# A macaron block on one core: each attention step's third maximum cut into two half-length pieces that share a bank, the two row halves of the array shifted against each other, and the transposed maxima sent to their rows by transfers inside SBUF

## The chip, the cores and the metric

The kernel runs on one core of a Trainium2 chip. The metric is the device time of one execution in microseconds (us); lower is better. Every profile that is shown is that of one execution.

## The reference

The block works on `x` of 4 batches x 1024 rows x 512 columns. It adds half of a feed-forward of the normalised rows, then attention of the normalised rows, then half of the same feed-forward again. What the change touches is the softmax of the attention (32 query heads, 8 key heads, 16 columns to a head, so 4 query heads to a key head):

```python
scores = jnp.einsum('bhqd,bhkd->bhqk', Q, K) / np.sqrt(HD).astype(np.float32)
w = jax.nn.softmax(scores, axis=-1)
attn = jnp.einsum('bhqk,bhkd->bhqd', w, V)
...
x = x + 0.5 * _L0_ffn_ref(_layernorm(x, axis=-1), L0_ffn_w_gate_up, L0_ffn_w_proj)
x = x + _L0_attn_ref(_layernorm(x, axis=-1), ...)
x = x + 0.5 * _L0_ffn_ref(_layernorm(x, axis=-1), L0_ffn_w_gate_up, L0_ffn_w_proj)
```

A softmax subtracts each row's maximum before it takes the exponential. The kernel computes the scores twice: once laid out with queries on the partitions, only to find each query's maximum, and once transposed, with keys on the partitions, for the exponential.

## The kernel before, in words

The program alternates between a feed-forward stage (`FeedForward`, its steps called pieces) and an attention stage for each of the four batches. Within both the order of instructions is written out by hand (`manual_schedule`); each engine then runs its own list in that order and waits on semaphores.

**The attention stage** is `Attention.run`. It has 128 steps per batch: 8 key heads `g`, for each two halves of the queries `qh`, for each eight tiles of 128 keys `kc`. One step `n` does this:

- `scores`, twice, for the head pairs 0 and 1 (the tiles `s`, L1273). Each pair is two TensorE matmuls with a contraction of 64 rows, 512 columns wide; one uses the upper 64 rows of the array, the other the lower 64, so that they run beside each other. The tile `s` of a pair has one place in PSUM, and the step of the next keys adds to what is there. So a pair's matmuls in step n+1 wait until the exponential of that pair in step n has read `s`. Where `kc` is 0, two more matmuls per pair add the negated maxima (`pick` times `even_rows` or `odd_rows`).
- the exponentials on ScalarE (the tiles `e`, L1282), one of 1024 columns per pair.
- three maxima for a key head that is computed later (`maxima`, tiles `sm`, L1138): a matmul with a 64-row contraction and 512 columns, and its reduction on VectorE (L1147). Two of them stand behind the first pair of scores, one in each row half. The third stands behind the second pair of scores, in one row half; the other half has nothing beside it.
- `weigh` (tiles `o`, L1289) for the step before: the exponentials times the values, four matmuls 32 columns wide, each in two passes.

**Where the maxima go.** Some of the maxima of a batch, 168 of 512, are computed in the feed-forward pieces ahead of its attention stage (`early`, in groups of four, up to the limit `EARLY`). When a key head has all of its maxima, VectorE reduces them to 32 numbers for each query row and splits these into two parts (`subtract_maxima`, L1169 to L1173). TensorE transposes them (`turn`, L1181), VectorE copies them out, GpSimd's queue writes them to DRAM (`d_m`, L1185) and reads them back as rows (`maxima_in`, L1221). The last two key heads take another way, without DRAM (`turn_half`): four transposes of 128x128 (L1208) and a copy of 512 columns (L1209), for four query tiles at a time.

**`divide`** ends a pair of key heads, 32 steps. The outputs `oT` go to DRAM (`d_o`), the denominators come back (`den`, on SyncE's queue). Three pieces of work then wait in the list `after`, and the step loop takes them out 7, 12 and 15 steps later: `invert` (VectorE's reciprocal, a write to `d_r`, and GpSimd's load of `aT` from `d_o`, L1085), `spread` (SyncE's load of `rec` from `d_r`, 512 KB, L1088) and `multiply` (GpSimd, `aT` times `rec`, L1091). With the first three `divide`s of a batch taken up in steps 32, 64 and 96, `multiply` is given out in steps 47, 79 and 111. The fourth is done behind the loop.

**Loads.** `Places` keeps four sets of three SBUF tiles for the queries and keys of a key head, one kind for maxima (`p_m`) and one for scores (`p_s`). `done` sets a place free, and the next load in a fixed order is issued on SyncE's queue, three transfers of 512 KB.

Of the kernel before, what the change touches and what calls it, by code (L numbers as in the profile page):

```python
# [19 lines left out]
P = 128  # L20
# [5 lines left out]
PAIR = 64  # L26
# [11 lines left out]
def tile_macaron_block(  # L38
# [21 lines left out]
    KV = HKV * HD  # L60

# [744 lines left out]
    def output(old, put, then, wp, ps):  # L806
        for i in range(NT):
            put.bias(i)
            put(i, range(DC - 1))
            if i == 3 or i == NT - 1:  # L810

                for _ in range(2 if i == 3 else 1):
                    old.after.pop(0)()
        turns = []
        for some in ([0, 1], [2, 3]):
            for i in some:
                put(i, range(DC - 1, DC))
            scales = normal_scales(then.tiles(0, some), f"last_{some[0]}")
            turns += then.normalize(0, some, wp, ps, "pa", 4, scales, NT)

        ends = []
        for i in range(4, NT):
            put(i, range(DC - 1, DC), ends)
        for step in turns + ends:
            step()

    def input_output(new, old, put, then, wp, ps):
        turn, banks = None, 2 if put is None else 1
        puts = {4: (0,), 5: (1,), 6: (2,), 7: (3,), 8: (4,), 9: (5, 6, 7)}
        for n in range(NT + 2):  # L830
# [40 lines left out]
            if put is not None and n == 3:  # L871
                old.after.pop(0)()
# [24 lines left out]
    class Attention:  # L897
# [19 lines left out]
        READY = (HKV - 1) * STEPS + NT - 3  # L917
        FIRST = 3
        EARLY = (3 * ITEMS - 4) * G

        def __init__(self, b):
            self.b = b


            self.d_q = dram.tile([D, 2, T], F32, tag="d_q", name=f"d_q_{b}", bufs=2)
            self.d_k = {
                kind: dram.tile([KV, 2, 2, T], F32, tag=f"d_k{kind}", name=f"d_k{kind}_{b}", bufs=2)
                for kind in "ms"
            }
            self.d_o = dram.tile([HQ, 2, HD, T], F32, tag="d_o", name=f"d_o_{b}", bufs=2)  # L930
            self.aT, self.after, self.when = {}, [], 0
            self.counts, self.ended = [0] * G, [0] * G
            self.pm, self.mT, self.mrows = {}, {}, {}
            self.early_rows = None
            self.rows, self.xTs, self.made = {}, {}, {}
            self.turning = []
# [132 lines left out]
        def divide(self, c, wp):  # L1069
# [20 lines left out]
            def multiply():  # L1090
                nc.gpsimd.tensor_tensor(a, a, rec, ALU.mult)  # L1091
                self.aT[c] = a

            self.after += [invert, spread, multiply]
# [31 lines left out]
        def maxima(self, j, ps, bufs):  # L1126

            g, n = divmod(self.counts[j], self.ITEMS)
            self.counts[j] += 1
            i, half = divmod(n, 2)  # L1130
            *q, k = places.at["m", self.b, g]
            if g not in self.pm:
                self.pm[g] = ring.tile([P, NT, G, 2], F32, tag="pm", name=f"pm_{self.b}_{g}")
            pm = self.pm[g]
            tag = "sm" if bufs < 4 else "gu"
            s = ps.tile([P, 512], F32, tag=tag, name=f"sm_{self.b}_{g}_{j}_{n}", bufs=bufs)
            at = slice(j % 2 * PAIR, (j % 2 + 1) * PAIR)
            nc.tensor.matmul(  # L1138
                s,
                lhsT=q[j // 2][at, i * P : (i + 1) * P],  # L1140
                rhs=k[at, half * 512 : (half + 1) * 512],
                start=True,
                stop=True,
            )

            def end():
                nc.vector.tensor_reduce(pm[:, i, j, half : half + 1], s, AX.X, ALU.max)  # L1147
                before = min(self.ended)
                self.ended[j] += 1
                done, rest = divmod(min(self.ended), self.ITEMS)  # L1150
                if min(self.ended) == before:
                    return
                if rest == self.ITEMS // 2 and g == HKV - 1:
                    self.turn_half(g, 0)
                elif rest == 0:
                    if g < HKV - 2:
                        self.subtract_maxima(g, ps, bufs)
                    else:
                        for part in range(g == HKV - 1, 2):
                            self.turn_half(g, part)  # L1160
                    places.done(("m", self.b, g))

            return end

        def subtract_maxima(self, g, ps, bufs):

            b = self.b
            m = small.tile([P, NT, G], F32, tag="m", name=f"m_{b}_{g}", bufs=2)
            nc.vector.tensor_reduce(m, self.pm[g], AX.X, ALU.max, negate=True)  # L1169
            mst = small.tile([P, G, 2, NT], F32, tag="mst", name=f"mst_{b}_{g}", bufs=2)  # L1170
            by_head = m.rearrange("p i j -> p j i")
            nc.vector.tensor_copy(mst[:, :, 0, :].bitcast(F32R), by_head)
            nc.vector.tensor_tensor(  # L1173
                mst[:, :, 1, :].bitcast(F32R), by_head, mst[:, :, 0, :], ALU.subtract
            )
            rows = G * 2 * NT
            tag = "sm" if bufs < 4 else "gu"

            def turn():
                pt = ps.tile([P, 512], F32, tag=tag, name=f"pmT_{b}_{g}", bufs=bufs)  # L1180
                nc.tensor.transpose(pt[:rows, :P], mst.rearrange("p j r i -> p (j r i)"), ident)  # L1181
                mrow = small.tile([rows, P], F32R, tag="mrow", name=f"mrow_{b}_{g}", bufs=2)
                nc.vector.tensor_copy(mrow, pt[:rows, :P])
                self.mT[g] = dram.tile([rows, P], F32, tag="d_m", name=f"d_m_{b}_{g}", bufs=HKV)
                nc.gpsimd.dma_start(self.mT[g], mrow.bitcast(F32))  # L1185
                if g == 0:
                    self.maxima_in(g)

            self.turning.append(turn)

        def turn_half(self, g, part):

            tiles = slice(part * 4, part * 4 + 4)
            m = small.tile([P, 4, G], F32, tag="m", name=f"m_{self.b}_{g}_{part}", bufs=2)
            nc.vector.tensor_reduce(m, self.pm[g][:, tiles], AX.X, ALU.max, negate=True)
            columns = self.spread[:, tiles].rearrange("p i (e s) -> p i e s", s=PAIR)[..., :4]
            high, low = (columns[..., r::2] for r in range(2))
            m = m.rearrange("p i (a e) -> p i e a", e=2)  # L1200
            nc.vector.tensor_copy(high.bitcast(F32R), m)
            nc.vector.tensor_tensor(low.bitcast(F32R), m, high, ALU.subtract)

            def turn():
                t = self.mrows[g] = self.odd_rows if g % 2 else even_rows
                pt = self.ps.tile([P, 512], F32, tag="sm", name=f"pmT_{self.b}_{g}_{part}", bufs=3)
                for i in range(4):
                    nc.tensor.transpose(pt[:, i * P : (i + 1) * P], self.spread[:, part * 4 + i, :], ident)  # L1208
                nc.vector.tensor_copy(t[:, part * 512 : (part + 1) * 512], pt)  # L1209

            self.turning += [None, turn] if g == HKV - 1 else [turn]

        def maxima_in(self, g):
# [5 lines left out]
            for j in range(G):  # L1219
                at = j % 2 * PAIR + j // 2 * 2  # L1220
                nc.gpsimd.dma_start(t[at : at + 2, :].bitcast(F32), flat[j])  # L1221

        def early(self, ps, share, more):
# [14 lines left out]
            if more and sum(self.counts) + G <= min(share, 1.0) * self.EARLY:  # L1238
                ends = [self.maxima(sum(self.counts) % G, ps, 4) for _ in range(G)]
# [10 lines left out]
        def run(self, keep, wp, ps):  # L1250
# [3 lines left out]
            self.spread = wp.tile([P, NT, P], F32, tag="spread", name=f"spread_{b}", bufs=1)  # L1254
# [4 lines left out]
            def scores(g, qh, kc, pair):  # L1259
# [10 lines left out]
                for n, (lhsT, rhs) in enumerate(terms):  # L1270
                    for e in range(2):
# [8 lines left out]
                        )  # L1280
                w = wp.tile([P, 2, 512], F32, tag="e", name=f"e_{name}", bufs=4)
                return w, lambda: nc.scalar.activation(w, s, AF.Exp, scale=1.0 / HD**0.5)  # L1282
# [27 lines left out]
            pattern = [((0, 1), (2,)), ((3, 0), (1,)), ((2, 3), (0,)), ((1, 2), (3,))]  # L1310
            more = (0, 5, 10, 15)
            late = None
            places.load(("t2", b + 1) if b + 1 < B else ("out", B))
            for n in range(HKV * self.STEPS):
# [3 lines left out]
                if n % self.STEPS > 0 and g + 1 < HKV and g + 1 in self.mT and g + 1 not in self.mrows:  # L1318
                    self.maxima_in(g + 1)
                if self.after and n in (self.when + 7, self.when + 12, self.when + 15):  # L1320
# [6 lines left out]
                sides = list(pattern[n % 4]) if n > 0 else [(), ()]  # L1327
                if n > 0 and n % 16 in more and self.TOTAL - sum(self.counts) > 3 * (self.READY - n):
                    sides[1] += (sides[1][0] ^ 1,)
                es, ends = {}, []  # L1330
                for pair, heads in enumerate(sides):
                    es[pair], end = scores(g, qh, kc, pair)
                    ends.append(end)
                    for j in heads:
                        if self.counts[j] < HKV * self.ITEMS:
                            ends.append(self.maxima(j, ps, 3))
                for end in ends:
                    end()
# [6 lines left out]
                if n == 1:  # L1345
                    nc.gpsimd.memset(self.spread, 0.0)
# [111 lines left out]
```

## Time and profile before

| | us |
|---|---|
| median of 3 runs | 3197.84 (3196.88 to 3199.02) |
| the profiled execution, its own time | 3200.95 |
| its span from the first to the last instruction | 3199.2 |
| TensorE busy in it | 3112.0 (97%) |
| VectorE, ScalarE, GpSimd busy | 2188.1, 1758.5, 951.0 |

How to read it: in the waits, "A <- B: total, times, longest" says that A's engine stood idle until B ended. A timeline line gives the start, the length and the instruction, merged with equal ones next to it (xN); what stands in brackets is the idle time ahead of it and who ended it. PE is TensorE's matmuls, PEld its weight loads, DVE VectorE, ACT ScalarE, POOL GpSimd, SP SyncE. The ends of matmuls are modelled and each overlaps the next, so what counts for TensorE is the distance from start to start. In a row of windows, each engine's busy time stands in this order: PE, PEld, DVE, ACT, POOL, then the granted clock of TensorE, the DMA share and GB/s.

### The profile page before, as it was taken

What the parts mean: (1) busy time and instruction counts of PE and PEld (TensorE: products, weight loads), DVE (VectorE), ACT (ScalarE), POOL (GpSimd) and SP (SyncE); (2) the same over time, 40 slices, a digit from 0 to 9 for tenths busy, and PEclk for the clock granted to TensorE, in tenths of its full rate; (3) what the DMA queues carried; (4) which work ended last, traced back from release to release, by engine and by line L of the source; (5) the groups of instructions that cost most, each with busy time, mean ns of one, the idle gap of its engine ahead of it and who ended that gap; (6) DMA issues with size and microseconds to landing.
All of it is one profiled execution on the core that took longest, in us unless ns stands there. A gap on an engine that the chain in (4) does not pass through costs nothing. (4 is left out here: it accounts for less than half of the span.)

```text
span 3199.2 us, 46128 instructions
## 1 busy us (share of the span) xinstructions
PE 3112.0 (97%) x16944; PEld 1963.6 (61%) x16944; DVE 2188.1 (68%) x3659; ACT 1758.5 (55%) x2346; POOL 951.0 (30%) x932
## 2 busy tenths in 40 slices
PE   5999899999999999999999999999999999999999
PEld 4777677733358777533377777433487776333687
DVE  7976566588855666688756665888556666887243
ACT  5752333389852333689823333898623335888343
POOL 2564333300034343201053333110243332010344
PEclk8999999999999999999999999999999999999999
DMA  3543222224324133133333222133241231332111
GB/s 111 161 125 97 88 61 78 62 76 120 111 82 129 53 93 109 45 117 102 91 107 96 87 73 70 70 110 115 86 130 60 76 96 61 97 120 65 41 60 42
DMA packets 229522, 285.64 MB, mean 89 GB/s; under 512 B 29296, under 2 KB 174704, under 8 KB 229296
## 3 DMA queue, kind: packets, MB, share of 16 engines
q1 hardware_dynamic: 220784, 271.66, 27.4%
q0 software_dynamic: 8512, 11.03, 1.6%
q8 instruction: 134, 2.20, 0.3%
q14 instruction: 92, 0.75, 0.1%
HBM read 215.74 MB, written 66.85 MB: 88 GB/s over the span
## 5 line engine op out<-in xcount | busy, mean ns | idle before, releaser
L1147 DVE TENSOR_REDUCE pm<-sm 128x1 f32<-128x512 f32 x2048 | 1281.1, 683 | 213.5 <-PE sm L1138 211.3
L1282 ACT ACTIVATE e<-s 128x1024 f32<-128x1024 f32 x1024 | 991.6, 1024 | 147.4 <-PE s L1273 138.9
L205 PE MATMUL gu<-xT,guT 128*128 128x512 f32 x1792 | 710.0, 396 | 9.9 <-DVE ql L1064 8.3
L205 PE MATMUL gu<-xL,guT 128*128 128x512 f32 x1792 | 703.2, 392 | 0.4 <-DVE xL L133 0.4
L1289 PE MATMUL o<-e,vs 128*32 128x512 f32 x4096 | 548.1, 604 | 0.0
L1138 PE MATMUL sm<-p_m,p_m 64*128 64x512 f32 x2048 | 497.1, 412 | 8.8 <-DVE h L217 6.0
L1273 PEld LDWEIGHTS s<-p_s,p_s 64*128 64x128 f32 x2048 | 193.0, 183 | 485.5 <-ACT e L1282 467.7
L1273 PE MATMUL s<-p_s,p_s 64*128 64x512 f32 x2048 | 469.0, 451 | 9.6 <-ACT e L1282 9.6
L225 POOL TENSOR_TENSOR sq<-h 128x512 f32<-128x512 f32 x210 | 218.5, 1041 | 724.1 <-DVE h L217 724.1
L217 DVE TENSOR_TENSOR h<-sg,gu 128x512 f32<-128x512 f32 x224 | 153.7, 686 | 381.2 <-PE gu L205 370.5
L215 ACT ACTIVATE sg<-gu 128x512 f32<-128x512 f32 x224 | 134.2, 599 | 480.6 <-PE gu L205 480.5
L205 PEld LDWEIGHTS gu<-xT,guT 128*128 128x128 f32 x1792 | 339.6, 190 | 84.9 <-ACT guT L94 8.7
L205 PEld LDWEIGHTS gu<-xL,guT 128*128 128x128 f32 x1792 | 339.4, 189 | 72.5 <-DVE xL L133 1.2
L245 PE MATMUL po<-w_pT,high 128*128 128x512 f32 x896 | 374.8, 418 | 0.7 <-DVE x L282 0.7
L245 PE MATMUL po<-w_pT,low 128*128 128x512 f32 x896 | 356.7, 398 | 0.2
L231 ACT CAST high<-h 128x512 fp32r<-128x512 f32 x224 | 139.1, 621 | 335.4 <-DVE h L217 323.5
L1138 PEld LDWEIGHTS sm<-p_m,p_m 64*128 64x128 f32 x2048 | 227.9, 185 | 93.9 <-DVE h L217 49.9
L229 POOL TENSOR_TENSOR acc<-acc,sq 128x512 f32<-128x512 f32 x205 | 275.8, 1346 | 16.0
L94 ACT CAST guT<-g 128x512 fp32r<-128x512 bf16 x448 | 275.0, 614 | 8.0 <-ACT guT L94 5.5
L245 PEld LDWEIGHTS po<-w_pT,high 128*128 128x128 f32 x896 | 168.7, 188 | 94.4 <-issue 56.4
L233 DVE TENSOR_TENSOR low<-h,high 128x512 fp32r<-128x512 f32 x224 | 168.6, 753 | 40.9 <-ACT high L231 40.9
L1289 PEld LDWEIGHTS o<-e,vs 128*32 128x32 f32 x4096 | 81.2, 108 | 180.9 <-issue 155.2
(166 smaller groups left out, 2934.9 us busy)
## 6 DMA issues: line engine op xcount, KB each, us to landing
g<-d_guT SPq DMA_DIRECT2D x448, 128.0 KB
p_m<-d_q SPq DMA_DIRECT2D x56, 512.0 KB
p_s<-d_q SPq DMA_DIRECT2D x56, 512.0 KB
d_o<-oT SPq DMA_DIRECT2D x64, 256.0 KB
p_m<-d_km SPq DMA_DIRECT2D x28, 512.0 KB
p_s<-d_ks SPq DMA_DIRECT2D x28, 512.0 KB
x<-in_L_attn_x_dram SPq DMA_DIRECT2D x32, 256.0 KB
w<-in_L_ffn_w_gate_up_dram SPq DMA_DIRECT2D x32, 256.0 KB
```

What stands on the lines that cost most here:

```text
L94: nc.scalar.copy(w, t)
L205: nc.tensor.matmul(pg, lhsT=self.weights[k, hc][part][:, c, :], rhs=xp[:, c, :], start=(c == 0 and low == 0), stop=(c == DC - 1 and low == 1),
L217: nc.vector.tensor_tensor(h, sg, gu[1], ALU.mult)
L225: nc.gpsimd.tensor_tensor(sq, h, h, ALU.mult)
L229: nc.gpsimd.tensor_tensor(acc, acc, sq, ALU.add)
L233: return (high, low), lambda: nc.vector.tensor_tensor(low, h, high.bitcast(F32), ALU.subtract)
L245: nc.tensor.matmul(self.pos[k][i], lhsT=h[:, i * P : (i + 1) * P], rhs=w_pT[hc], start=(hc == 0 and n == 0), stop=(hc == HC - 1 and n == 1),)
L1138: nc.tensor.matmul(s, lhsT=q[j // 2][at, i * P : (i + 1) * P], rhs=k[at, half * 512 : (half + 1) * 512], start=True, stop=True,)
L1147: nc.vector.tensor_reduce(pm[:, i, j, half : half + 1], s, AX.X, ALU.max)
L1273: nc.tensor.matmul(s[:, e, :], lhsT=lhsT[at], rhs=rhs[at, queries], start=(kc == 0 and n == 0), stop=(n == len(terms) - 1), skip_group_che ...
L1282: return w, lambda: nc.scalar.activation(w, s, AF.Exp, scale=1.0 / HD**0.5)
L1289: nc.tensor.matmul(o[j * SLOT : (j + 1) * SLOT, :], lhsT=vs[:, kc, g, :], rhs=es[j // 2][:, j % 2, :], start=(kc == 0), stop=(kc == NT - 1),)
```

## The change

**The third maximum.** `counts` now goes by quarters of 256 keys and by pairs of heads. Per step one pair gives three quarters of its row: two as a whole 512-column matmul in each row half (`maxima`, here called the large ones), and the third as two 256-column matmuls, one in each row half, that write the two halves of one PSUM bank (`two_quarters`, the small ones). One reduction takes both small ones.

**The order on TensorE** within a step becomes: small in the lower row half; large in the upper; scores of pair 0, lower half first; large in the lower half; small in the upper half; scores of pair 1; `weigh`. The row halves so run with an offset of 256 columns.

**A dependency by way of GpSimd.** The two small matmuls of a step must not write their bank at the same time. `two_quarters` puts an instruction without work (`nop`) in GpSimd's list: it waits for the first small matmul, and the second waits for it. In the built program this is an event of GpSimd's sequencer, 452 in all, each standing in GpSimd's list at the place of its step.

**The rest.** `multiply` is cut into four pieces of 256 columns, given out 15, 16, 17 and 18 steps after `divide`. From key head 3 on, the transposed maxima go from `mrow` straight to their rows, four transfers on SyncE's queue; `turn_half` and its tile `spread` are gone, and the last two key heads are done in halves of four query tiles. For key heads 3 to 6 the three VectorE steps ahead of the transpose are given out one per step (`chores`). The rows of key heads 1 and 2 are still read back from DRAM, now on SyncE's queue. `EARLY` grows by 8: in the built program 168 maxima of the first batch and 172 of each other are computed in the feed-forward pieces.

```diff
-        EARLY = (3 * ITEMS - 4) * G
+        EARLY = (3 * ITEMS - 4) * G + 8
...
-            def multiply():
-                nc.gpsimd.tensor_tensor(a, a, rec, ALU.mult)
+            def multiply(n):
+                some = slice(n * T // 4, (n + 1) * T // 4)
+                nc.gpsimd.tensor_tensor(a[:, some], a[:, some], rec[:, some], ALU.mult)
                 self.aT[c] = a
 
-            self.after += [invert, spread, multiply]
+            self.after += [invert, spread] + [lambda n=n: multiply(n) for n in range(4)]
...
+        def two_quarters(self, pair, ps):
+            place = self.take(pair, 1)
+            g, i, quarter = place
+            name = f"sm_{self.b}_{g}_{pair}_{i}_{quarter}"
+            s = ps.tile([P, 2, QUARTER], F32, tag="sm", name=name, bufs=3)
+            made = []
+
+            def begin(e):
+                made.append(self.maximum(s[:, e, :], pair, e, place, 1))
+                if len(made) == 1:
+                    made.append(nc.gpsimd.nop())
+                sync = mybir.DependencyInfo(mybir.DependencyClass.Sync, mybir.DependencyReason.DATA)
+                tc.add_manual_dep(made[-1].ins, made[-2].ins.name, sync, reason="one bank, two row tiles")
+
+            def end():
+                to = self.pm[g][:, i, 2 * pair : 2 * pair + 2, quarter]
+                nc.vector.tensor_reduce(to, s, AX.X, ALU.max)
+                self.end(pair, 1, ps, 3)
+
+            return begin, end
...
-                self.mT[g] = dram.tile([rows, P], F32, tag="d_m", name=f"d_m_{b}_{g}", bufs=HKV)
-                nc.gpsimd.dma_start(self.mT[g], mrow.bitcast(F32))
-                if g == 0:
-                    self.maxima_in(g)
+                if g < self.FIRST:
+                    self.mT[g] = dram.tile([rows, P], F32, tag="d_m", name=f"d_m_{b}_{g}", bufs=HKV)
+                    nc.gpsimd.dma_start(self.mT[g], mrow.bitcast(F32))
+                    if g == 0:
+                        self.maxima_in(g, nc.gpsimd)
+                    return
+                t = self.mrows[g] = self.odd_rows if g % 2 else even_rows
+                for j in range(G):
+                    at = j % 2 * PAIR + j // 2 * 2
+                    nc.sync.dma_start(
+                        t[at : at + 2, first * P : (first + n) * P].bitcast(F32),
+                        mrow[j * 2 * n : (j + 1) * 2 * n, :].bitcast(F32),
+                    )
...
-                if self.after and n in (self.when + 7, self.when + 12, self.when + 15):
+                if self.after and n - self.when in (7, 12, 15, 16, 17, 18):
                     self.after.pop(0)()
...
+                if small:
+                    small[0](1)
+                if large:
+                    large[0][0]()
+                begins[0](0)
+                if kc == 0:
+                    begins[0](1)
+                exps[0]()
+                if large:
+                    large[0][1]()
+                    large[1][0]()
+                if small:
+                    small[0](0)
+                    small[1]()
+                if large:
+                    large[1][1]()
+                begins[1](0)
+                if kc == 0:
+                    begins[1](1)
+                exps[1]()
+                if self.chores:
+                    self.chores.pop(0)()
                 if late is not None:
                     weigh(*late)
                 if turn is not None:
                     turn()
```

## The prediction

> **What bounds the kernel now.** I read the waits first, for who stands idle on whom.
>
> ```profile
> PEld s L1273 <- ACT e L1282: 467.7, 787, 1.1
> POOL aT L1091 <- DMA rec<-d_r: 247.5, 15, 27.7
> DVE pm L1147 <- PE sm L1138: 211.3, 552, 1.5
> ACT e L1282 <- PE s L1273: 138.9, 412, 7.1
> ```
>
> In the attention stage the weight loads of the scores wait on the exponential, and the exponential in turn on the scores: a loop of the two. `multiply` (L1091) waits long for `rec`; nobody waits for it now. Next, the timeline of one ordinary step.
>
> ```profile
> 2753.28 0.39 PE L1138 MATMUL sm<-p_m,p_m 64*128 64x512 f32 x2
> 2753.51 0.40 PE L1273 MATMUL s<-p_s,p_s 64*128 64x512 f32 x2
> 2753.55 1.94 ACT L1282 ACTIVATE e<-s 128x1024 f32<-128x1024 f32 x2 [0.19 <-PE s L1273]
> 2753.75 0.39 PE L1138 MATMUL sm<-p_m,p_m 64*128 64x512 f32 x1
> 2754.07 1.07 PE L1289 MATMUL o<-e,vs 128*32 128x512 f32 x8
> 2755.06 0.50 PE L1273 MATMUL s<-p_s,p_s 64*128 64x512 f32 x2
> 2755.66 1.02 ACT L1282 ACTIVATE e<-s 128x1024 f32<-128x1024 f32 x1 [0.18 <-PE s L1273]
> ```
>
> One step is the distance between equal rows, 2751.95 to 2754.07 for `o`: 2.12 us. TensorE's starts in it are 0.34 + 0.23 + 0.24 + 0.32 + 0.99, so the third maximum holds 0.24 alone (a 512-column slot is 0.23). ScalarE works 1.94 and idles 0.18, VectorE reduces for 1.89. The loop through ScalarE: an exponential ends near 2753.36, pair 1's scores start at 2753.51, third maximum 2753.75, `o` 2754.07, pair 0's scores 2755.06, exponential 2755.66: 2.30 after the first end. Plus a pair of exponentials, 1.95, that is 4.25 for two steps, again 2.12. So two loops of one length hold the step.
>
> The last steps of a stage have no maxima at all. The windows, in order PE, PEld, DVE, ACT, POOL, clock:
>
> ```profile
> 2957.31:2969.80 12.49, 11.44 (x77) 3.18 (x74) 0.00 (x0) 12.02 (x14) 0.00 (x0) 1.00 0.06 21
> 3004.00:3012.00 8.00, 5.24 (x17) 3.82 (x18) 6.13 (x12) 1.07 (x2) 0.70 (x1) 0.70 0.01 2
> ```
>
> The first row is six steps without VectorE: 12.49/6 = 2.08 us each, ScalarE busy 12.02 of 12.49. Taking maxima off TensorE cannot bring a step below that.
>
> **Part 1, the half slot.** The change takes 0.24 out of one place and 0.115 of TensorE's time per step. But it puts a large maximum, 0.23, in the row half of pair 0's scores ahead of them, in the loop through ScalarE. That loop stays within 0.01. TensorE's loop falls to about 2.00; the second small matmul must wait for the first (256 columns, about 0.28 from the record's length) plus an event there and back (0.04 + 0.05) plus a weight load, some 0.06 too late, so 2.05. The longer loop rules: 2.12, floor 2.08. I take 4 ns off 452 steps, -2 us; the ends are -18 (0.04 x 452, the floor) and, if the two loops add, +45 (0.10 x 452).
>
> **Part 2, the event in GpSimd's list.** Each of 113 steps per batch has an event in GpSimd's sequencer, in order. The second small matmul waits for it; behind that matmul on TensorE stand pair 1's scores and `o`, behind those ScalarE. `multiply` is given out before the step's event. Where does its wait stand?
>
> ```profile
> L1091 POOLq EVENT_SEMAPHORE  x16: 17/17/17, 745.2 to 2992.4; - x16
> ```
>
> All sixteen `multiply`s have such an event on GpSimd's sequencer (POOLq), the first at 745.2, when `rec` landed. While it waits, the sequencer passes nothing on. Steps 47 and 79 of the first batch, `o` against `multiply`:
>
> ```profile
> 740.42 1.07 PE L1289 MATMUL o<-e,vs 128*32 128x512 f32 x8
> 745.37 2.38 POOL L1091 TENSOR_TENSOR aT<-aT,rec 128x1024 f32<-128x1024 f32 x1 [26.98 <-DMA rec<-d_r]
> 811.43 1.06 PE L1289 MATMUL o<-e,vs 128*32 128x512 f32 x8
> 825.50 2.38 POOL L1091 TENSOR_TENSOR aT<-aT,rec 128x1024 f32<-128x1024 f32 x1 [17.31 <-DMA rec<-d_r]
> ```
>
> `rec` is late by 4.95 and 14.07. Over the four batches step 47 gives 4.95 + 6.18 + 6.26 + 5.23 = 22.6, step 79 gives 14.07 + 11.97 + 12.28 + 11.20 = 49.5. In step 111 it is about 6 us early (880.08 against 886.20): nothing. The lateness comes from the queue: `d_r` and `rec` follow three loads of 512 KB (the window 730 to 738 shows 50 GB/s), and the change leaves that. The small matmul stands 0.4 ahead of `o`, eight times 3; the four row transfers of key head 3, now on SyncE's queue ahead of loads, 2 in the first batch, 0 to 5. Sum +77. The wait of L1085's loads for `d_o` (steps 39, 71, 103) has 3.5 us or more in hand, so nothing.
>
> The rule that speaks against this stall: the Trainium skill's "Perfetto Trace Analysis", section "GPSIMD Engine Instruction", lets an instruction wait in a queue of its own while the sequencer fetches the next one. By it the events would pass the waiting `multiply` and the 77 would be 0. The event row above decides for me: here the wait is the sequencer's own.
>
> **Part 3, the clock behind a stall.** TensorE stands still 5 to 14 us, eight times. After an idle of 2.91:
>
> ```profile
> 3005.88 0.87 PE L130 MATMUL pxn<-ident,xn 128*128 128x128 f32 x6 [2.91 <-DVE xn L119]
> 3013.07 0.63 PE L205 MATMUL gu<-xL,guT 128*128 128x512 f32 x1
> 3013.50 0.63 PE L205 MATMUL gu<-xT,guT 128*128 128x512 f32 x1
> 3014.22 0.39 PE L205 MATMUL gu<-xT,guT 128*128 128x512 f32 x1
> 3014.44 0.39 PE L205 MATMUL gu<-xL,guT 128*128 128x512 f32 x1
> ```
>
> The distance is 0.43 until 3014.2, then 0.22: half speed for 8.3 us, and the window 3004 to 3012 above has the clock at 0.70. After an idle of 8.32 (from 321.04) it was 5.2 us. Half speed costs 44% of 5 to 8 us where TensorE's work is 88% of the step's length, 2.3 to 3.6 per stall. I take 2.5, eight times: +20, between 0 (clock stays up) and 29.
>
> The Trainium skill's "TensorE: Matmul & The Clock Gate", Part 1, has the array at half clock after one idle window of about 3.4 us and at full clock after about 3.4 us of work: estimated from that page, 1.5 to 3.0 per stall and 12 to 24 in all. The rows differ from it: 2.91 idle was enough here, and 8.3 and 5.2 us passed before full speed.
>
> **Part 4, bursts taken away.** Distances of `o` beyond 2.12 (2.58 where `kc` is 0), per batch: the ends of key heads cost 0.29 + 0.83 + 0.83 + 0.29 + 0.15 + 0.73 and the last 0.4 (three VectorE steps of 0.2 in a row, then late reductions), the rows' wait near step 80 costs 0.6, and `turn_half` in steps 94 to 96, where `o` stands at 2896.12, 2899.23, 2903.02 and 2905.88, costs 2.9. Together 7.0. After: eight turns of about 0.3 and two heads whose three steps stay together, 1.2, so 3.6. Times 4: -13, between -28 (all gone) and 0 (the row transfers bring new waits). `multiply` in pieces moves nothing: nobody waits for it inside the loop. The rows' transfers move from GpSimd's queue to SyncE's, four issues of about 0.6 per key head; behind them stand key loads and `den`, which have more than a step in hand but for the first batch's +2 of part 2. VectorE's work stays three reductions of 512 columns per step, so its 0.24 of idle stays.
>
> **Part 5, early maxima.** Three batches compute one more group of four in the feed-forward, where TensorE is 9 tenths busy in nearly every slice: four slots less the gap they fill, 0.86 each (603.10 to 604.19, less 0.23), +3.
>
> **Sum**: 77 + 20 - 13 + 3 - 2 = +85. The profiled execution took 3200.95 us of its own (span 3199.2), 0.1% over the median 3197.84, so the sum is put on the median: **3282 us**.
>
> **Rivals.** *Step shorter, stall kept*: if TensorE's 0.115 came through whole, 452 x 0.115 = 52 less, 3232. For it: TensorE's 97% busy. Against it: the 2.08 floor. *Events pass the waiting multiply, or `rec` comes in time*: parts 2 and 3 vanish, 3198 - 13 + 3 - 2 = 3186, faster. Its place is GpSimd's sequencer in steps 47 and 79; it decides once the eight stalls together fall below some 10 us, that is an average lateness near 1 instead of 9.6. The four pieces give `multiply` no more time, since the first waits for all of `rec`. *Both*: no stalls and 0.115 a step, 3134; at the floor, 3170. *The change does not do what it says*: the offset of the row halves is not kept, so that the round trip of the event lies bare between the small matmuls and the loops add; 0.10 to 0.23 more per step, 3327 to 3386. For it: `sm` and `s` already take 0.34 and 0.32 where one slot is 0.23.
>
> **Chances.** The forecast 0.72; the shorter step with stalls 0.08; loops adding 0.07; no stalls 0.07; both 0.04; terms that cancel 0.02. About 0.2%, 6.4 us, is what a measurement of this kernel can tell from no change. Faster: 0.07 + 0.04 = 0.11. Same: 0.02. Slower: 0.87. For the range: low end, the forecast without clock loss and with step and bursts at their good ends (-20 - 16 - 15 = -51), 3231, taken to 3225 so that the shorter step lies in it; high end, clock 29, bursts 0, and half of the +45: 3282 + 9 + 13 + 24 = 3328.
>
> **What would show it.** Right: TensorE idle 5 to 7 us ahead of an `sm` in step 47 and 11 to 15 in step 79 of each batch, ended by GpSimd; `multiply`'s event at the same moment; the clock low behind each; `o` every 2.12 otherwise; no 3-us steps near 94. Wrong: `sm` never waiting on GpSimd for more than 0.2 (then 3186 or less), or `o` at 2.0 or at 2.2 and more throughout.

## The result, and the profile after

The changed kernel takes 3274.48 us (median of 4 runs, 3272.70 to 3276.32) against 3198.43 before: 1.0237 times as long, 95% interval 1.022 to 1.0255. The forecast was 3282, range 3225 to 3328. The profiled execution took 3275.63 us of its own, 74.7 more than that of before.

Five lines of the waits of the changed kernel (who <- whom: total, times, longest):

```profile
PEld sm L1141 <- DVE pm L1189: 299.3, 357, 0.8
POOL aT L1093 <- DMA rec<-d_r: 278.1, 12, 30.2
ACT e L1332 <- PE s L1322: 185.6, 241, 11.6
PEld s L1322 <- ACT e L1332: 69.1, 141, 0.8
PE sm L1141 <- POOLq L1183: 63.7, 8, 11.4
```

The last line is new. L1183 is the event without work, POOLq is GpSimd's sequencer, and eight times TensorE stood still for it, 63.7 us together. Step 79 of the first batch, on all engines:

```profile
831.47 1.41 POOL L1093 TENSOR_TENSOR aT<-aT,rec 128x256 f32<-128x256 f32 x2 [29.71 <-DMA rec<-d_r]
831.80 0.28 PEld L1141 LDWEIGHTS sm<-p_m,p_m 64*128 64x128 f32 x1 [11.51 <-POOLq L1183]
831.80 0.58 PE L1141 MATMUL sm<-p_m,p_m 64*128 64x256 f32 x1 [11.20 <-POOLq L1183]
832.90 1.02 ACT L1332 ACTIVATE e<-s 128x1024 f32<-128x1024 f32 x1 [11.38 <-PE s L1322]
```

`multiply` starts at 831.47, when `rec` has landed; 0.33 later the second small matmul starts, and behind it the scores and the exponential, which idled as long. The events show the order in step 47 too: `multiply`'s own event passes on GpSimd's sequencer at 747.67, the event without work right behind it at 747.77, and the second small matmul starts at 747.84. The clock behind this stall, in windows (PE, PEld, DVE, ACT, POOL, clock, DMA share, GB/s):

```profile
831.80:838.00 6.20, 6.20 (x27) 2.89 (x31) 3.27 (x5) 2.63 (x3) 1.80 (x3) 0.50 0.01 1
838.00:846.00 8.00, 8.00 (x64) 3.26 (x56) 6.05 (x10) 6.95 (x9) 0.74 (x1) 0.97 0.47 170
```

For the 6.2 us of the first row, and 0.4 more, TensorE works at half clock; then full speed comes back. An ordinary step is no shorter than the 2.12 that it was; the distances of `o` alternate between 2.22 and 2.03, mean 2.125:

```profile
1373.77 1.06 PE L1339 MATMUL o<-e,vs 128*32 128x512 f32 x8
1375.59 1.94 ACT L1332 ACTIVATE e<-s 128x1024 f32<-128x1024 f32 x2 [0.32 <-PE s L1322]
1375.80 1.06 PE L1339 MATMUL o<-e,vs 128*32 128x512 f32 x8
```

And one wait that the sum had left at nothing, in step 104 of the first batch:

```profile
894.63 0.89 PE L1322 MATMUL s<-even_rows,pick 64*128 64x512 f32 x2 [4.81 <-DMA even_rows<-mrow]
```

Another stands behind the last step of each of the first three batches, where the normalised rows of the next batch are transposed (`pxn_a`): 3.41 to 3.49 of idle. The first of them, with its place in the kernel before (first line) and in the changed one:

```profile
924.50 0.63 PE L130 MATMUL pxn_a<-ident,xn_a 128*128 128x128 f32 x4 [1.10 <-DVE xn_a L119]
953.73 0.66 PE L131 MATMUL pxn_a<-ident,xn_a 128*128 128x128 f32 x4 [3.49 <-ACT axT_a L132]
```

ScalarE's copy `axT_a`, which it waits for, itself waits 2.80 for the write of the last outputs (`d_o<-oT`), which it did not in the kernel before. Run 10 below has the same wait, so it belongs to the part of the change without the cut; why the copy waits is not tested.

### The profile page after: what moved, and what is told of

It reads as the page before. It is cut to its first block, busy times and chain, and to the rows that moved or that the text cites. A ratio compares the mean times of both kernels' runs of the same rounds, so it can differ in the third digit from the quotient of the medians.

```text
span 3273.8 us, 47523 instructions
## 1 busy us (share of the span) xinstructions
PE 3120.3 (95%) x17348; PEld 2013.0 (61%) x17348; DVE 2187.2 (67%) x3659; ACT 1758.3 (54%) x2346; POOL 906.7 (28%) x884
## 5 line engine op out<-in xcount | busy, mean ns | idle before, releaser
L1162 DVE TENSOR_REDUCE pm<-sm 128x2 f32<-128x512 f32 x1596 | 1049.2, 685 | 217.4 <-PE sm L1141 198.9
L1141 PEld LDWEIGHTS sm<-p_m,p_m 64*128 64x128 f32 x2500 | 284.8, 185 | 550.8 <-DVE pm L1189 299.3
L1141 PE MATMUL sm<-p_m,p_m 64*128 64x256 f32 (+1 forms) x2500 | 556.4, 417 | 69.9 <-POOLq L1183 63.7
L1339 PE MATMUL o<-e,vs 128*32 128x512 f32 x4096 | 556.8, 613 | 0.0
L1322 PE MATMUL s<-p_s,p_s 64*128 64x512 f32 x2048 | 496.6, 428 | 7.5 <-ACT e L1332 6.7
L1189 DVE TENSOR_REDUCE pm<-sm 128x2 f32<-128x512 f32 x452 | 309.2, 684 | 76.3 <-PE sm L1141 76.1
L1322 PEld LDWEIGHTS s<-p_s,p_s 64*128 64x128 f32 x2048 | 213.1, 188 | 87.7 <-ACT e L1332 69.1
```

The lines of the kernel that those rows point to most:

```text
L1141: return nc.tensor.matmul(s, lhsT=q[pair][at, i * P : (i + 1) * P], rhs=k[at, quarter * QUARTER : (quarter + n) * QUARTER], start=True, st ...
L1162: nc.vector.tensor_reduce(to, s, AX.X, ALU.max)
L1189: nc.vector.tensor_reduce(to, s, AX.X, ALU.max)
L1322: nc.tensor.matmul(s[:, e, :], lhsT=lhsT[at], rhs=rhs[at, queries], start=(kc == 0 and n == 0), stop=(n == len(terms) - 1), skip_group_che ...
L1339: nc.tensor.matmul(o[j * SLOT : (j + 1) * SLOT, :], lhsT=vs[:, kc, g, :], rhs=es[j // 2][:, j % 2, :], start=(kc == 0), stop=(kc == NT - 1),)
```

## The experiments

Theory A is that of the prediction: the events stand in GpSimd's list behind `multiply`'s wait for `rec`. Theory B is that the cut of the third maximum and its event cost the time themselves, wherever `multiply` stands. Runs 2, 3, 4, 6 and 7 are one execution each.

**1. `multiply` later.**

```diff
-                if self.after and n - self.when in (7, 12, 15, 16, 17, 18):
+                at_steps = (7, 12, 24, 25, 26, 27) if self.when < 96 else (7, 12, 15, 16, 17, 18)
+                if self.after and n - self.when in at_steps:
```

> The changed kernel with the four pieces of multiply given out 24 to 27 steps after divide in place of 15 to 18 (first two divides of a batch; the third keeps 15 to 18). Theory A, the events are held up behind multiply's wait for rec: the eight idles of TensorE (63.7 us in the changed kernel's trace) and the half clock behind them (about 22) vanish, 3274 - 86 = 3188 us, which is faster than before. Theory B, the loss lies in the cut of the third maximum itself (its event's round trip, smaller pieces, a step that adds up): multiply's place is of no account, 3274 within 5.

Measured: 3226.23 us, 1.0085 times before (1.0068 to 1.0102). The eight idles are gone, so B falls. But the gain is 48 us, not 86: in step 80 of each batch a wait of 5.7 to 6.6 us has come up for the rows of key head 5.

```profile
819.88 0.89 PE L1322 MATMUL s<-odd_rows,pick 64*128 64x512 f32 x2 [6.11 <-DMA odd_rows<-mrow]
```

In the changed kernel these rows landed while TensorE stood still for `multiply`'s sake in step 79: two waits at one place, of which only the longer showed. SyncE's timeline says why they are late:

```profile
796.41 1.29 SPq L750 DMA_DIRECT2D p_m<-d_q  x2
797.75 0.52 SPq L750 DMA_DIRECT2D p_m<-d_km  x1
...
804.74 3.73 SPq L1235 DMA_DIRECT2D odd_rows<-mrow  x4
```

The four small transfers are issued by 808.5, behind 1.5 MB of queries and keys in the same queue. The trace has no landing time for them; the matmul that waits for them starts at 819.88, 11 us after the last issue.

**2. `multiply` four steps later.** The same line with 19 to 22.

> The changed kernel with multiply's pieces given out 19 to 22 steps after divide, four steps (8.7 us) later. Theory A: the step-47 idles (9.05, 3.45, 3.69, 2.74 in the changed kernel) go but for 0.4 in the first batch, the step-79 idles (11.20, 11.08, 11.42, 11.07) shrink to about 2.5 each; 3274 less 63.7 - 10.4 = 53 of idle and half of the clock loss, about 3210 us. Theory B: 3274 within 5. A third view, that rec's lateness follows multiply's own place (later multiply, later rec): the idles stay.

Measured: 3223.43 us. The step-47 idles are gone but for a step of 3.29 in the first batch; those of step 79 are not 2.5 but are taken over by the rows' wait of step 80, 5.1 to 7.0. So this run can't show how much of the idle in step 79 the four steps would take away; it shows that `rec` doesn't follow `multiply`.

**3. The event in another engine's list.**

```diff
-                    made.append(nc.gpsimd.nop())
+                    made.append(nc.scalar.nop())
```

> The changed kernel with the event in ScalarE's list in place of GpSimd's; multiply stays at steps 47 and 79. Theory A: the events no longer stand behind multiply, so that the eight idles vanish as in the run with the late multiply, about 3188 us; a few us more if an event holds up an exponential. Theory B: the round trip stays, 3274 within 5.

Measured: 3228.33 us, the same as the late `multiply`, with the same rows' wait in step 80 (5.8 to 6.9) and not one of the eight idles. `multiply` stands where it stood and waits as before, while TensorE goes on:

```profile
742.29 1.06 PE L1339 MATMUL o<-e,vs 128*32 128x512 f32 x8
744.33 1.07 PE L1339 MATMUL o<-e,vs 128*32 128x512 f32 x8
746.97 2.81 POOL L1093 TENSOR_TENSOR aT<-aT,rec 128x256 f32<-128x256 f32 x4 [26.30 <-DMA rec<-d_r]
```

So the stall needs both: `multiply`'s wait, and the event behind it in the same list. Take away either (runs 1 and 3) and it is gone.

**4. The event alone, on the kernel before.** `maxima` makes the event behind the step's first maximum, and the third waits for it:

```diff
+                if event == 1:
+                    self.event = nc.gpsimd.nop()
+                    tc.add_manual_dep(self.event.ins, mm.ins.name, sync, reason="event")
+                elif event == 2 and self.event is not None:
+                    tc.add_manual_dep(mm.ins, self.event.ins.name, sync, reason="event")
```

> The kernel before with one thing added: in each step an event in GpSimd's list waits for the first of the step's maxima, and the step's third maximum waits for the event. No maximum is cut, no order on TensorE is changed; the rows read back from DRAM go through SyncE's queue, so that they don't stand in GpSimd's list. Theory A: multiply's waits in steps 47 and 79 now stop TensorE here too, by the lateness in the trace of before and the clock behind it: 3198 + 72 + 20 = 3290 us (3270 to 3305). Theory B: an event alone, with nothing cut, costs nearly nothing, 3198 to 3205.

Measured: 3339.57 us, 50 more than A expected and outside both ranges. The stalls are there (steps 47 and 79, 2.1 to 9.4 of idle each, shorter than expected; the steps ahead of them are longer, which leaves `rec` more time), but the ordinary steps have grown too, from 2.12 to 2.36:

```profile
2803.00 0.39 PE L1282 MATMUL s<-p_s,p_s 64*128 64x512 f32 x2
2803.37 0.18 PEld L1139 LDWEIGHTS sm<-p_m,p_m 64*128 64x128 f32 x1 [0.41 <-issue]
2803.40 0.46 PE L1139 MATMUL sm<-p_m,p_m 64*128 64x512 f32 x1
```

Here nothing stands between the scores and the third maximum to cover the event's way to GpSimd and back, and the start is 0.40 after the scores where it was 0.24; another 0.08 comes behind it. In the some 390 steps of four batches that begin no new row of keys (where `kc` is 0 the distance grew by 0.03 only) 0.24 makes 94 us. This is not the price of the changed kernel's event: here the weights of the third maximum wait for two things, and the second wait stands as an event on TensorE's own sequencer (444 of them; the changed kernel has none for its event), so that the weights come 0.11 after GpSimd's event, against 0.05 there. In the changed kernel the two small matmuls start 0.57 apart. The first one's record takes 0.38 of it and the event's way, from the end of that record to the second one's weights, 0.10, so that it stays hidden.

**5. The rows on another queue.** The late `multiply`, the event on ScalarE, and

```diff
-                    nc.sync.dma_start(
+                    nc.gpsimd.dma_start(
                         t[at : at + 2, first * P : (first + n) * P].bitcast(F32),
```

> The late multiply (24 to 27 steps), the event in ScalarE's list, and the four transfers of the rows on GpSimd's queue in place of SyncE's. In the late-multiply run what is left of the stalls is a wait for the rows: in step 80 of each batch about 6 us, in step 104 of the first batch 4.3, some 40 us with the half clock behind them. Theory A: two waits stood at one place, multiply's hid the rows' one; with the rows on a queue that no key load and no denominator stands ahead of, both are gone: 3226 - 40 = 3186 us, faster than before. Rival: the transfers share the 16 DMA engines with the key loads whatever queue issues them, and land as late: 3226.

Measured: 3187.38 us, 0.9964 times before (0.9951 to 0.9978), 0.4% less. No idle of TensorE over 1.2 us is left between the first and the last step of any attention stage. Since the late `multiply` and the event on ScalarE each left the rows' wait as it was (runs 1 and 3; the two together were not run), what took it away was the other queue. The four transfers of the first batch's key head 5, issued from 801.95, landed by 810.0, 6 us after the last issue and 0.4 ahead of the matmul that reads them:

```profile
801.95 2.22 POOL L1235 DMA_DIRECT2D odd_rows<-mrow  x4 [20.35 <-DVE mrow L1225]
```

That fits the Trainium skill's "DMA: Bandwidth & Descriptors", whose section "Queues, rings and completion order" has each DMA engine go round its queues packet by packet; no run here shows the turns themselves.

**6. and 7. What holds the step.** Two cuts, both on the late `multiply`: the small pair's reduction on half of its columns, and exponentials on half of theirs.

```diff
-                nc.vector.tensor_reduce(to, s, AX.X, ALU.max)
+                nc.vector.tensor_reduce(to, s[:, :, :128], AX.X, ALU.max)
```

> The late-multiply kernel (3226 us) with VectorE's reduction of the small pair reading 128 of each 256 columns, so that half of the third maximum is left out of the maxima: VectorE has some 0.27 us less per step. The prediction's reason, that the loop through ScalarE holds the step: nothing changes, 2.12 per step, 3226. The rival, read from the waits of the changed kernel (the weights of the first small matmul wait 0.84 for VectorE's reduction, in most steps), that VectorE and the three places of sm hold it: the step falls to the 2.08 of the steps without maxima or below, 3208 or less.

```diff
-                return w, begin, lambda: nc.scalar.activation(w, s, AF.Exp, scale=1.0 / HD**0.5)
+                return w, begin, lambda: nc.scalar.activation(w[:, :, :256], s[:, :, :256], AF.Exp, scale=1.0 / HD**0.5)
...
-                        rhs=es[j // 2][:, j % 2, :],
+                        rhs=es[j // 2][:, j % 2, :256].unsqueeze(1).to_broadcast([P, 2, 256]),
```

> The late-multiply kernel (3226 us) with each exponential on half of its columns and weigh reading that half twice: the other half of the exponentials is left out, ScalarE has about 0.9 us less per step, TensorE the same work. If the loop through ScalarE holds the step, it falls to TensorE's loop, 2.00 to 2.05, that is 3226 less 452 x 0.07 to 0.12, 3172 to 3195. If VectorE and the places of sm hold it, it stays at 2.12: 3226 within 6.

Measured: 3228.57 with the shorter reduction, no change beside 3226.23; 3187.97 with the shorter exponentials, 38 less, the steps at 2.03 and 2.10. Two steps of that run:

```profile
1380.56 1.09 ACT L1332 ACTIVATE e<-s 128x512 f32<-128x512 f32 x2 [0.95 <-PE s L1322]
1380.84 1.06 PE L1339 MATMUL o<-e,vs 128*32 128x512 f32 x8
1381.83 0.18 PEld L1141 LDWEIGHTS sm<-p_m,p_m 64*128 64x128 f32 x2 [0.84 <-DVE pm L1189]
```

ScalarE now idles 0.95 a step, and the step falls to 2.065: the loop through ScalarE holds it at 2.125. What holds the 2.065 is not parted: TensorE's own loop (2.05 in the sum) fits, but VectorE is busy 1.88 of it, and in one of the two steps the weights of a large maximum wait 0.14 for it. The wait of 0.84 for VectorE, the first line of the waits shown above, is no loss: it is the weight loader's, while the eight matmuls of `o` run, and the same 0.84 stood ahead of the scores before the change.

**8. and 9. Another order, to shorten ScalarE's loop.** The fifth run's kernel with pair 0's scores first:

```diff
-                if small:
-                    small[0](1)
-                if large:
-                    large[0][0]()
                 begins[0](0)
...
                 exps[0]()
+                if small:
+                    small[0](1)
                 if large:
+                    large[0][0]()
                     large[0][1]()
```

> The kernel with the rows on GpSimd's queue (3187 us), and within a step pair 0's scores ahead of the first small and the first large maximum, no longer behind them; then small, large, large, small, pair 1's scores, weigh. If the loop through ScalarE holds the step, as the half exponentials showed, this takes 0.23 out of the way from pair 1's scores to the next exponential of pair 0, that is 0.115 per step, and TensorE's own loop (2.065 in the run with half exponentials) becomes the bound: 452 x 0.06 = 27 less, 3160 us. Rival: the two small matmuls now stand 256 columns closer, so that the event's round trip (0.24 where it lay bare) shows by 0.1 or more, and the step stays at 2.12 or above: 3187 to 3230.

> The same with the second small matmul behind pair 1's scores, just ahead of weigh, and the second large maximum's reduction behind the small one's: the event has its time, but 0.115 to 0.2 (the last small matmul has nothing beside it in the other row half) stand in ScalarE's loop again. ScalarE's loop then gives about 2.07, TensorE's about 2.10: 3175, between 3160 and 3190.

Measured: 3247.58 (1.0151, 1.0135 to 1.0166) and 3206.93 us (1.0025, 1.0015 to 1.0034). Both expectations of a gain were wrong. The first's rival named the right cause with too small a price (3187 to 3230): its step is 2.25 throughout, and the second small matmul waits for the event:

```profile
1373.50 0.76 PE L1141 MATMUL sm<-p_m,p_m 64*128 64x256 f32 x4
1373.88 0.18 PEld L1141 LDWEIGHTS sm<-p_m,p_m 64*128 64x128 f32 x1 [0.19 <-ACTq L1183]
```

It starts 0.38 after the first, which is the first one's record, 0.28, and the event's way, 0.10. With the small one last it is 2.15 and 2.21, still longer than the 2.125 of the changed kernel's order. The waits of that run don't part what of it is the event and what is the lost offset of the row halves.

**10. The other half of the change alone.** The kernel before with the transfers to the rows inside SBUF (on GpSimd's queue), `turn_half` gone, the last two key heads in halves, the VectorE steps one per step, `EARLY` 8 more; no cut, no event. One piece of the edit:

```diff
-                if rest == self.ITEMS // 2 and g == HKV - 1:
-                    self.turn_half(g, 0)
+                if rest == self.ITEMS // 2 and g >= HKV - 2:
+                    self.subtract_maxima(g, ps, bufs, 0)
```

> The kernel before with only the second half of the change: the transposed maxima of key heads 3 to 7 go to their rows by transfers inside SBUF (on GpSimd's queue), the last two key heads in halves, the three VectorE steps one per step, EARLY 8 more. The third maximum stays whole, the order on TensorE and multiply stay as before, there is no event. By the sum of the prediction: bursts -13, early maxima +3, 3188 us, so that the cut of the third maximum is worth nothing beside it (3187 with both). Rival: the cut itself gives the gain of the 3187 kernel, and this one stays at 3198.

Measured: 3190.76 us, 0.997 times before (0.9959 to 0.998). Beside the 3187.38 with the cut (0.9951 to 0.9978) the two intervals overlap: what the cut itself is worth lies under what these runs can tell apart, and the gain is that of the second half of the change.

## Why the prediction was right, point by point

The total moved by 74.7 where the sum had 85. Taken apart by the distances of `o`, against the same kind of step where nothing waits:

| | sum | measured |
|---|---|---|
| TensorE idle for the event, eight stalls | +77 | +63.7 |
| longer steps behind them, put down to the half clock (the stalled steps and the next one or two are 83.5 longer; less 63.7) | +20 | +19.8 |
| wait for the rows, step 104 of the first batch | 0 | +7.5 |
| bursts (what is left of the four attention stages' +69.4) | -13 | -14.3 |
| ordinary steps (0.13 less in 8, 56 times) | -2 | -7.3 |
| all outside the attention stages | +3 | +5.3 |
| sum | 85 | 74.7 |

The main term and its mechanism were right. That the total came within 11 us is in part luck: the stall and the steps came out 19 us below their terms, and a wait for rows that had no term, with the rest, put some 8 back.

- **Part 2, the stall**, carries the result, and runs 1, 3 and 4 show it: it goes away with a later `multiply`, goes away with another list for the event, and comes with the event. Its size was 13 us too large. Step 79 measured 11.07 to 11.42 where 11.2 to 14.07 and 0.4 stood in the sum; step 47 2.74 to 3.69 in the later batches where 5.2 to 6.3 stood, and 9.05 in the first, where 7.4 did. So none of the four step-47 idles lies in the 5 to 7 us that were named as the sign. The lateness of `rec` was read off the trace of before, in which its load was issued elsewhere: in the changed kernel it follows the four row transfers in step 79 (issued from 817.87, behind 813.61 to 817.76). Why the lateness came out smaller is not taken apart.
- **The Trainium skill's "Perfetto Trace Analysis", section "GPSIMD Engine Instruction"** would have had the events pass the waiting `multiply`. The event row of before decided against it, and 11.20 us of TensorE's idle ended by the event, 0.33 after `multiply`'s start, agrees with the row, as do the events at 747.67 and 747.77.
- **Part 3, the clock**: 20 was right, 2.5 per stall; the window shows half clock for 6.2 us, and even the shortest idle, 2.74 in the fourth batch, had 1.9 of longer steps behind it. The Trainium skill's "TensorE: Matmul & The Clock Gate", Part 1, with 12 to 24 by its figures, holds for the sum. Its 3.4 us of idle does not fit: 2.74 was enough. Its 3.4 us for the way back is the short end here: the clock stood at 0.50 for 3.4 us behind the idle of 2.74, and for 6.6 behind the 11.20 shown above.
- **Part 1, the step**: the reason holds. The loop through ScalarE keeps 2.125 (runs 6 and 7), and the step without it measured 2.065 where the sum had 2.05 for TensorE's loop. The event's way, put at 0.09, measured 0.10 (the changed kernel and run 8). The -2 us came out as -7.3. The floor of 2.08 was misread: one of its six steps begins a row of keys, and the others alternate between 1.83 and 2.19, about 2.01 for a pair, so that the good end of -18 was drawn too near; nothing came of it here.
- **Parts 4 and 5, the bursts and all outside**: the totals are close, the pieces are not. Run 10 without the cut is 3199.47 - 3190.76 = 8.7 us net, where -13 and +3 make 10; but in its profile the attention stages are 18.7 shorter and all outside them is 7.9 longer. In the changed kernel's +5.3 the early maxima don't show: the new wait for `axT_a` and the slow projections behind it make some 12 us over three batches, the feed-forward pieces that follow are some 5 shorter although they hold the added maxima, and the two ends of the run 1.6 shorter. Why these pieces are shorter stays open. (The 0.86 of part 5 ends at a weight load, 604.19; the matmul starts at 604.09, which gives 0.76.) And the sentence in part 4 on SyncE's queue failed: the rows didn't have more than a step in hand. Step 104 of the first batch shows it openly, and step 80 of all batches once the longer wait is gone (runs 1, 2 and 3).
- **The rival without stalls**, 3186, needs the rows' wait gone too: with the stalls alone taken away it is 3226 (slower than before), and only with the rows on another queue 3187. The stalls with the longer steps behind them added 83.5, and their removal gave back 48.
- *Step shorter* and *the row halves don't keep their offset* did not come true in the changed order; run 8 shows the event's way lying bare in another order, at 0.13 per step.

## What to carry to other kernels

A dependency that goes by way of a third engine's list takes over every wait that stands in that list ahead of it: before adding one, read which waits of that engine nobody minds today, and how late they end against the step. When a wait is taken away, look for what was due in its shadow; two waits at one place cost only the longer, and the shorter gets its full price afterwards. A freed half slot on the busiest engine is worth next to nothing when a second loop of the same length, here through ScalarE, does not pass through it.

## What the runs showed of the hardware

- An event on GpSimd's sequencer stood behind the wait of an arithmetic instruction ahead of it in the list, and held up TensorE for up to 11.42 us (the changed kernel). In ScalarE's list, between exponentials of 1 us, it ended no idle of TensorE over 1.2 us (runs 3 and 5).
- From the end of a matmul's record to an event on GpSimd's sequencer it took 0.04 us, and from the end of the event to the next matmul's weights 0.05 (the changed kernel; the same through ScalarE in run 8). Where the weights wait for something else too and nothing covers the event, a step of 2.12 became 2.36 (run 4).
- Behind 1.5 MB of loads on SyncE's queue, the matmul that waited for four transfers to a few rows started 11 us after the last of them was issued (run 1); from GpSimd's queue beside the same loads they landed 6 us after the last issue (run 5).
- The granted clock of TensorE fell to 0.50 behind an idle of 2.74 us and stayed there for 3.4 (the changed kernel).
